# Gated cross-attention with RMS norm on one core: where the last quad's element-wise work and the first quad's weight sums stand in the engines' queues

## The chip, the cores and the metric

The kernel runs on one core of a Trainium2 chip. The metric is the device time in microseconds (us) of one launch; the median of three runs is given, and one further execution was recorded by the profiler. Five engines matter. TensorE (PE in the profile) multiplies matrices, and its weight loads have a row of their own (PEld). VectorE (DVE) and ScalarE (ACT) work element by element and can read the accumulators (PSUM). GpSimd (POOL) works element by element on SBUF. SyncE (SP) issues DMA transfers. Each engine works through its own queue in order, and waits there for what other engines have to finish.

## The reference

```
memory_proj = einsum('bme,de->bmd', memory, W_mem)
scores = einsum('bnd,bmd->bnm', x, memory_proj) / sqrt(D)
memory_context = einsum('bnm,bmd->bnd', softmax(scores), memory_proj)
gate = sigmoid(einsum('bnf,df->bnd', concat([x, memory_context]), W_gate) + b_gate)
fused = x + gate * memory_context
out = fused * rsqrt(mean(square(fused)) + 1e-6) * norm_w
```

Here x is 8 x 1024 x 1024, memory is 8 x 64 x 512, D is 1024, and everything is float32. The first half of W_gate (called W1) is multiplied with x; the second half acts on the attention's output, and its product with memory_proj is made once in a setup stage.

## The kernel before

The 8192 rows of x are taken in 16 groups of 512 rows, here called quads (`NQ` = 16), each of four tiles of 128 rows. The product of a quad with W1 is made as seven smaller products (a Strassen scheme on two levels), in the order 1, 6, 7, 5, 4, 2, 3 of `ORDER` (line 584). Each of the seven is one call of `outer_product` (line 726) and is itself made of seven inner products, called A, B, C, D, A again, E and F. Each inner product is one slot, so a quad has 49 slots. The last four outer products (5, 4, 2, 3) also carry a part of the attention's output and of the gate (`ext`): between the second A and E, TensorE multiplies the attention weights with the memory (tiles pc, and sums into kA, kF, kE and kD).

What comes out of PSUM is taken out as follows. ScalarE copies A to p1 (line 783). VectorE adds B, C and D to make u2, u3 and u4 (lines 785, 787, 791). GpSimd adds u3 and u4 to the gate tiles (`pre`, line 765), and VectorE adds A, D, E and F (`fin`, line 771). In the four products with `ext`, ScalarE then makes the sigmoid of two half tiles of 128 x 512: d, the odd tile of a row pair, after E, and c, the even one, after F. TensorE needs the copy p1 before the second A may add to the same bank, since it adds to what it left there, and it needs u4 before the attention product may add to D's bank.

Work beside these products stands in a table by slot: `at(slot, fn)` (line 577) enters it, and `step()` (line 628) issues what is due right before the slot's inner product. Within one slot, what was entered first is issued first. The order so written is kept on each engine (`pin`). Thus a step that is moved by one slot changes its place in the queues of VectorE and ScalarE against the copies and sums of that slot, and never the order on TensorE.

For the first 15 quads, the product with the memory context is `gated` (line 633); adding x comes from a DMA that accumulates (`residual`), and `square` and `norm` (lines 647 and 660) follow in the next quad. The last quad has no next one, and differs. Its x lies in SBUF as xl. `last_gated` (line 691) multiplies a half tile with pc (which carries the memory context), adds xl, and ScalarE squares it with a sum along the row into one column of `halves` (`junk` takes the squares). `last_root` (line 704) adds the two half sums on VectorE and takes the root on ScalarE; `last_norm` (line 709) takes the reciprocal once per tile, scales a half tile and stores it. In the last quad rows 2 and 3 are finished by products 5 and 4, and rows 0 and 1 by products 2 and 3. Sigmoid and root lie in different tables of ScalarE, so a root between sigmoids has a table load ahead of it and one behind it (rows ACT_TABLE_LOAD); `sqrt_table` (line 721) loads the root's table early in the very end.

The first quad has a part of its own. Four sums of W1 each for products 2 and 3 (`inner_sum`, line 210, 128 x 512 each) are made on VectorE while the first quad runs, at the slots of line 625. Product 2 first needs its sums in slot 36, and product 3 in slot 43. The softmax of the first quad stands in the slots 10 (`softmax_a`) and 13 (`softmax_b`), and slot 18 transposes its result on TensorE (`transpose_attn`, tile pa).

Of the kernel before, what the change touches and what calls it, by code (L numbers as in the profile page):

```python
# [9 lines left out]
AF = mybir.ActivationFunctionType  # L10
ALU = mybir.AluOpType
# [4 lines left out]
P = 128  # L16
# [4 lines left out]
def tile_gated_cross_attention_rmsnorm(  # L21
# [42 lines left out]
    nc = tc.nc  # L64
    B, N, D = x.shape
# [18 lines left out]
    small = ctx.enter_context(tc.tile_pool(name="small", bufs=1))  # L84
# [9 lines left out]
    def tt(eng, o, a, b, op):  # L94
        pin(eng.tensor_tensor(o, a, b, op))  # L95
# [4 lines left out]
    def t4k(pool, shape, tag, name):  # L100
        return pool.tile(shape, F32, tag=tag, name=name)
# [475 lines left out]
    def at(slot, fn, *args):  # L577
        due.setdefault(slot, []).append(lambda: fn(*args))
# [43 lines left out]
    for o in (2, 3):  # L622
        w1_place(o)
    for i, (o, n) in enumerate((o, n) for o in (2, 3) for n in range(4)):
        at((3, 4, 5, 6, 10, 11, 12, 13)[i], inner_sum, nc.vector, o, n)
    slot = 0

    def step():
# [62 lines left out]
    def last_gated(t, h, pc):  # L691
        q = NQ - 1
        gated(q, t, h, pc)
        cols = slice(h * H, (h + 1) * H)
        g = O[q, t][:, cols]
        tt(nc.vector, g, g, xl[t][:, cols], ALU.add)
        if t not in halves:
            halves[t] = t4k(small, [P, 3], f"halves{t}", f"halves{t}")
        junk = t4k(small, [P, H], "junk", f"junk_{t}_{h}")
        pin(  # L700
            nc.scalar.activation(junk, g, AF.Square, accum_out=halves[t][:, h : h + 1])
        )

    def last_root(t):
        ss = halves[t]
        tt(nc.vector, ss[:, 2:3], ss[:, 0:1], ss[:, 1:2], ALU.add)
        pin(nc.scalar.activation(ss[:, 2:3], ss[:, 2:3], AF.Sqrt, bias=eps_sb, scale=1.0 / D))

    def last_norm(t, h):
        b, n0 = where(NQ - 1, t)  # L710
        rstd = halves[t][:, 2:3]
        if h == 0:
            pin(nc.vector.reciprocal(rstd, rstd))
        cols = slice(h * H, (h + 1) * H)
        g = O[NQ - 1, t][:, cols]
        pin(
            nc.vector.scalar_tensor_tensor(g, g, rstd, nw_sb[:, cols], ALU.mult, ALU.mult)  # L717
        )
        load(out[b, n0 : n0 + P, cols], g)
# [6 lines left out]
    def outer_product(q, o, ext):  # L726

        nonlocal slot, banks
        l11, l12, l21, l22 = quarters(left(q, o))
        s1, s2, s3, s4 = (L2[q, o][:, i, :, :] for i in range(4))  # L730
        kb = {}

        def product(name, tag, lhsT, s, start=True):
            nonlocal slot
            step()
            if name not in kb:
                kb[name] = ps.tile([P, C], F32, tag=banks[tag], name=f"k{name}{q}_{o}")
            for k in range(2):
                mm(kb[name], lhsT[:, k, :], w_op(o, s)[:, k, :], start and k == 0, k == 1)
            slot += 1  # L740

        def o_blocks(row, h):

            for t in (2 * row, 2 * row + 1):
                if (q, t) not in O:
                    O[q, t] = t4k(gpool, [P, D], "gate", f"gate{q}_{t}")
            return [
                O[q, 2 * row + r][:, h * H + n * C : h * H + (n + 1) * C]
                for r in range(2)
                for n in range(2)  # L750
            ]


        sums = {
            1: [(o_blocks(0, 0), None)],
            6: [(o_blocks(0, 1), (0, 0))],
            7: [(o_blocks(1, 0), (0, 1))] if o == 7 else [],
            5: [(o_blocks(1, 1), (1, 0)), (o_blocks(0, 1), (0, 1))] if o == 5 else [],
            4: [(o_blocks(1, 0), (1, 0))] if o == 4 else [],
            2: [(o_blocks(0, 0), (0, 0))] if o == 2 else [],  # L760
            3: [(o_blocks(0, 1), (0, 1))] if o == 3 else [],
        }[o]
        sums = [(dst, src and o_blocks(*src)) for dst, src in sums]

        def pre(n, u):

            for dst, src in sums:
                if src is not None:
                    tt(nc.gpsimd, dst[n], src[n], u, ALU.add)

        def fin(n, name, u):
            for dst, src in sums:
                if src is not None:
                    tt(nc.vector, dst[n], (src if u is None else dst)[n], kb[name], ALU.add)
                elif u is not None:
                    tt(nc.vector, dst[n], u, kb[name], ALU.add)
                else:
                    pin(nc.scalar.copy(dst[n], kb[name]))

        ut = t4k(rot, [P, 4, C], "u", f"u{q}_{o}")  # L780
        p1, u2, u3, u4 = (ut[:, i, :] for i in range(4))
        product("A", 0, l11, R11)
        pin(nc.scalar.copy(p1, kb["A"]))  # L783
        product("B", 1, s2, T2)
        tt(nc.vector, u2, p1, kb["B"], ALU.add)
        product("C", 2, s3, R12)
        tt(nc.vector, u3, u2, kb["C"], ALU.add)
        pre(3, u3)
        pre(2, u3)
        product("D", 3, s1, T1)  # L790
        tt(nc.vector, u4, u2, kb["D"], ALU.add)
        pre(1, u4)
        product("A", 0, l12, R21, False)
        pcs = []
        if ext:
            row, h, g = ext
            at_, mg = attnTs[q], mgs[q // QPB]
            for n in ("E", "F"):
                kb[n] = ps.tile([P, C], F32, tag=banks[4 if n == "E" else 1], name=f"k{n}{q}_{o}")
            for r, names in ((0, ("A", "F")), (1, ("E", "D"))):  # L800
                pc = ps_ctx.tile([P, H], F32, tag="ctx", name=f"pc{q}_{o}_{r}")
                for n in range(2):
                    cols = slice(h * H + n * C, h * H + (n + 1) * C)
                    mm(
                        pc[:, n * C : (n + 1) * C],
                        at_[0:M, 2 * row + r, :],
                        mg[0:M, cols],
                        n == 0,
                        True,
                    )  # L810
                    mm(
                        kb[names[n]],
                        at_[M:P, g + r, :],
                        mg[M:P, cols],
                        names[n] in "EF",
                        True,
                    )
                pcs.append(pc)
        for fn in beside.pop((q, o), ()):
            fn()  # L820
        fin(0, "A", None)
        fin(3, "D", u3)
        product("E", 4, l22, T4, not ext)
        fin(2, "E", u3)
        if ext:
            sigmoid(q, 2 * row + 1, h)
            last = q + 1 == NQ
            if last:
                at(slot + 1, last_gated, 2 * row + 1, h, pcs[1])
            else:  # L830
                at(slot + 1, gated, q, 2 * row + 1, h, pcs[1])
        product("F", 1, s4, R22, not ext)
        fin(1, "F", u4)
        if ext:
            sigmoid(q, 2 * row, h)
            if last:
                at(slot + 2, last_gated, 2 * row, h, pcs[0])
            else:
                at(slot + 2, gated, q, 2 * row, h, pcs[0])
        if o in (4, 3) and q + 1 == NQ:  # L840
            c, d = 2 * ext[0], 2 * ext[0] + 1
            if o == 3:
                sqrt_table()
            first = (4, 5) if o == 4 else (3, 3)
            at(slot + first[0], last_root, d)
            at(slot + first[1], last_root, c)
            for i, t in enumerate((d, c)):
                for h_ in range(2):
                    at(slot + first[1] + 1 + 2 * i + h_, last_norm, t, h_)
        elif o in (4, 3):  # L850

            row = ext[0]
            c, d = 2 * row, 2 * row + 1
            for t in (d, c):
                at(slot + 5, residual, q, t)
            if row == 0:
                when = (17, 18, 23, 29, None, None)
            else:
                when = (17, 18, 23, 25, 26, 28)
            at(slot + when[0], square, q, c)  # L860
            at(slot + when[1], square, q, d)
            for w_, (t, h_) in zip(when[2:], ((c, 0), (c, 1), (d, 0), (d, 1))):
                if w_ is None:
                    mid((q + 1, 4), norm, q, t, h_)
                else:
                    at(slot + w_, norm, q, t, h_)
        banks = [banks[i] for i in (2, 3, 0, 4, 1)]
        del L2[q, o]
# [34 lines left out]
```

## Time and profile before

| what | value |
|---|---|
| median of 3 runs | 979.76 us (979.5 to 979.79) |
| the profiled execution, its own time | 979.91 us |
| its span, first to last instruction | 978.1 us |
| mean granted clock of TensorE | 0.997 |
| first quad, TensorE | about 82.7 to 137.5 us |
| last quad, TensorE | about 909.2 to 967.5 us |
| last instruction on VectorE ends | 974.96 us |
| VectorE busy from 939.5 us to the end | 30.7 us |
| ScalarE, GpSimd busy in that stretch | 16.4 us, 15.0 us |

All times inside the kernel are counted from the first instruction of the profiled execution. In a line of the timeline, the first number is the start of a group of like instructions, the second is what it spans, and a number in brackets at the end is idle time of that engine ahead of it, with what ended it. A wait says which engine and tile waited, for whom, how long in total, how often, and the longest. An engine that is idle and isn't the bottleneck costs nothing.

### The profile page before, as it was taken

The numbers are of one execution on the slowest core, as the hardware profiler recorded it, in microseconds if no ns is written. First come the engines' busy times: TensorE is split into PE (matmuls) and PEld (weight loads), VectorE is DVE, ScalarE is ACT, GpSimd is POOL, SyncE is SP. The second block draws the span as 40 slices with busy tenths as digits, with TensorE's granted clock in tenths as the row PEclk, the third lists the DMA queues.
The fourth block names the chain that finished last, engine by engine and source line by source line (L and its number), as shares of the span: only waits on it lengthen the run. The fifth ranks groups of instructions, "written<-read, shape, count | busy, mean of one in ns | idle before, by whom it ended". The sixth has DMA issues, their size and how long they took to land.

```text
span 978.1 us, 14392 instructions
## 1 busy us (share of the span) xinstructions
PE 964.3 (99%) x4986; PEld 776.3 (79%) x4986; DVE 827.0 (85%) x1487; ACT 323.0 (33%) x596; POOL 754.6 (77%) x895
## 2 busy tenths in 40 slices
PE   9999999999999999999999999999999999999995
PEld 8646888888888888888888888888888888888873
DVE  5988788979797988979797988979797988979787
ACT  1000234151423334151423334151423334151434
POOL 4986878878787878878787878878787878878772
PEclk9999999999999999999999999999999999999998
DMA  9856173482818373482819373482818373482612
GB/s 371 267 147 157 27 130 98 114 177 72 176 65 174 117 130 98 112 179 73 176 65 175 113 131 99 112 180 71 177 66 172 116 133 98 111 181 68 169 65 86
DMA packets 71255, 128.32 MB, mean 131 GB/s; under 512 B 12432, under 2 KB 49296, under 8 KB 70928
## 3 DMA queue, kind: packets, MB, share of 16 engines
q1 hardware_dynamic: 61760, 93.34, 35.1%
q0 software_dynamic: 9280, 33.56, 18.6%
q8 instruction: 39, 0.64, 0.3%
q10 hardware_dynamic: 144, 0.52, 0.2%
q14 instruction: 32, 0.26, 0.1%
HBM read 87.56 MB, written 39.85 MB: 130 GB/s over the span
## 4 chain that ended last, share of the span: by engine, by line
PE 95%; DVE 3%; DMA 1%; issue 0%; ACT 0%; POOL 0%; DVEq 0%; ACTq 0%
PE kA L92 19%; PE pc L92 12%; PE kE L92 11%; PE kF L92 10%; PE kD L92 10%; PE kC L92 10%; PE kB L92 10%; PE psT L92 6%; PE pg L92 5%; PE pm L92 3%; DVE gate L95 1%; DMA memq<-in_mem 1%; DVE gate L717 0%; PE pa L427 0%; PE sc L401 0%
## 5 line engine op out<-in xcount | busy, mean ns | idle before, releaser
L95 POOL TENSOR_TENSOR gate<-gate,u 128x256 f32<-128x256 f32 x336 | 270.3, 834 | 116.0 <-DVE u L95 110.4
L639 ACT ACTIVATE gate<-gate 128x512 f32<-128x512 f32 x128 | 79.0, 629 | 400.7 <-DVE gate L95 400.6
L95 POOL TENSOR_TENSOR l<-a 128x256 f32<-128x256 f32 x128 | 128.6, 1004 | 56.3 <-DVE a L95 55.5
L333 DVE STREAM_TRANSPOSE a<-xq 128x512 f32<-128x512 f32 x128 | 138.0, 1100 | 3.2 <-DMA mgd<-mpq 3.2
L92 PE MATMUL pc<-mg,attnT 64*128 64x256 f32 x512 | 127.4, 389 | 0.0
L668 DVE SCALAR_TENSOR_TENSOR gate<-gate,ss,nw_sb 128x512 f32<-128x512 f32 x120 | 126.2, 1061 | 1.1
L92 PE MATMUL kD<-it,l 128*128 128x256 f32 x448 | 115.0, 379 | 0.0
L92 PE MATMUL kB<-it,l 128*128 128x256 f32 x448 | 115.0, 379 | 0.0
L92 PEld LDWEIGHTS pc<-mg,attnT 64*128 64x128 f32 x512 | 90.6, 186 | 29.7 <-issue 21.2
L92 PE MATMUL kA<-w,a 128*128 128x256 f32 x384 | 98.7, 379 | 0.4 <-ACT u L783 0.4
L92 PEld LDWEIGHTS kD<-it,l 128*128 128x128 f32 x448 | 85.1, 190 | 11.6
L92 PEld LDWEIGHTS kB<-it,l 128*128 128x128 f32 x448 | 85.1, 190 | 11.6
L95 DVE TENSOR_TENSOR gate<-gate,pc 128x512 f32<-128x512 f32 x128 | 87.2, 681 | 5.8 <-ACT gate L639 5.8
L95 POOL TENSOR_TENSOR l<-s 128x256 f32<-128x256 f32 x96 | 75.6, 787 | 10.1 <-PE kF L92 10.0
L92 PEld LDWEIGHTS kA<-w,a 128*128 128x128 f32 x384 | 71.6, 190 | 10.2 <-ACT u L783 0.8
L783 ACT COPY u<-kA 128x256 f32<-128x256 f32 x112 | 40.5, 362 | 102.4 <-PE kA L92 100.4
L95 DVE TENSOR_TENSOR u<-u,kB 128x256 f32<-128x256 f32 x112 | 45.6, 407 | 28.2 <-PE kB L92 24.7
L92 PE MATMUL kE<-it,a 128*128 128x256 f32 x256 | 69.0, 392 | 0.0
L92 PE MATMUL kA<-t,s 128*128 128x256 f32 x256 | 67.4, 386 | 0.0
L92 PE MATMUL kF<-w,l 128*128 128x256 f32 x256 | 65.7, 379 | 0.0
L92 PE MATMUL kC<-w,l 128*128 128x256 f32 x256 | 65.7, 379 | 0.0
L653 ACT ACTIVATE junk<-gate 128x1024 f32<-128x1024 f32 x60 | 63.5, 1059 | 1.4 <-DMA gate<-in_x 0.5
(138 smaller groups left out, 2034.2 us busy)
## 6 DMA issues: line engine op xcount, KB each, us to landing
xq<-in_x SPq DMA_DIRECT2D x64, 512.0 KB, 9.7
gate<-in_x POOLq DMA_DIRECT2D x60, 512.0 KB, 8.2
out<-gate SPq DMA_DIRECT2D x60, 512.0 KB, 2.6
w<-in_w_gate_t SPq DMA_DIRECT2D x8, 512.0 KB, 11.0
w<-in_w_gate_t SPq DMA_DIRECT2D x2, 2048.0 KB, 17.0
mg<-mgd SPq DMA_DIRECT2D x16, 256.0 KB, 3.8
mpd<-mpT SPq DMA_DIRECT2D x4, 512.0 KB, 6.5
mgd<-mpq SPq DMA_DIRECT2D x16, 128.0 KB, 4.4
```

The lines of the kernel that those rows point to most:

```text
L92: pin(nc.tensor.matmul(o, lhsT, rhs, start=start, stop=stop, skip_group_check=True))
L95: pin(eng.tensor_tensor(o, a, b, op))
L333: nc.vector.transpose(A[key][:, :, r * P : (r + 1) * P], chunks(xq[q][:, 4 * t : 4 * t + 4, :], KD)[:, half * KH : (half + 1) * KH],)
L639: pin(nc.scalar.activation(g, g, AF.Sigmoid))
L653: nc.scalar.activation(junk, O[q, t], AF.Square, accum_out=ss[:, t % 2 : t % 2 + 1])
L668: nc.vector.scalar_tensor_tensor(g[:, cols], g[:, cols], rstd[:, t % 2 : t % 2 + 1], nw_sb[:, cols], ALU.mult, ALU.mult,)
L783: pin(nc.scalar.copy(p1, kb["A"]))
```

## The change

There are two parts.

In the first quad, the four sums of W1 for product 3 move from the slots 10 to 13 to the slots 22 to 25. The four for product 2 stay.

In the last quad, every `last_gated` comes one slot later: d's moves from the slot of the next product's A to that of its B, and c's from C to D. `halves` keeps which half tile came first. After the square of the first half, ScalarE makes (sum / D + eps) with one more instruction of a single column (Identity), and the root takes that column as its bias and the second half's sum as its input, so VectorE's sum of the two halves falls away. The root of d is issued before the square of c in the very end. The four norms of rows 2 and 3, which stood in four slots one after the other, stand in the slots of A, C, the second A and E of the last product, 3 (offsets 7, 9, 11 and 12, where they were 6 to 9); the roots stay at 4 and 5. For rows 0 and 1, which come after the last product, the offsets only set the order.

The instructions of TensorE, of GpSimd and of the DMA queues keep their number and order. VectorE has four instructions fewer, ScalarE four more; the number of table loads is the same.

```diff
--- before.py
+++ after.py
@@ -622,7 +622,7 @@
     for o in (2, 3):
         w1_place(o)
     for i, (o, n) in enumerate((o, n) for o in (2, 3) for n in range(4)):
-        at((3, 4, 5, 6, 10, 11, 12, 13)[i], inner_sum, nc.vector, o, n)
+        at((3, 4, 5, 6, 22, 23, 24, 25)[i], inner_sum, nc.vector, o, n)
     slot = 0
 
     def step():
@@ -695,20 +695,29 @@
         g = O[q, t][:, cols]
         tt(nc.vector, g, g, xl[t][:, cols], ALU.add)
         if t not in halves:
-            halves[t] = t4k(small, [P, 3], f"halves{t}", f"halves{t}")
+            halves[t] = t4k(small, [P, 3], f"halves{t}", f"halves{t}"), h
+        ss, first = halves[t]
         junk = t4k(small, [P, H], "junk", f"junk_{t}_{h}")
+        pin(nc.scalar.activation(junk, g, AF.Square, accum_out=ss[:, h : h + 1]))
+        if h == first:
+            pin(
+                nc.scalar.activation(
+                    ss[:, 2:3], ss[:, h : h + 1], AF.Identity, bias=eps_sb, scale=1.0 / D
+                )
+            )
+
+    def last_root(t):
+        ss, first = halves[t]
+        h = 1 - first
         pin(
-            nc.scalar.activation(junk, g, AF.Square, accum_out=halves[t][:, h : h + 1])
+            nc.scalar.activation(
+                ss[:, 2:3], ss[:, h : h + 1], AF.Sqrt, bias=ss[:, 2:3], scale=1.0 / D
+            )
         )
-
-    def last_root(t):
-        ss = halves[t]
-        tt(nc.vector, ss[:, 2:3], ss[:, 0:1], ss[:, 1:2], ALU.add)
-        pin(nc.scalar.activation(ss[:, 2:3], ss[:, 2:3], AF.Sqrt, bias=eps_sb, scale=1.0 / D))
 
     def last_norm(t, h):
         b, n0 = where(NQ - 1, t)
-        rstd = halves[t][:, 2:3]
+        rstd = halves[t][0][:, 2:3]
         if h == 0:
             pin(nc.vector.reciprocal(rstd, rstd))
         cols = slice(h * H, (h + 1) * H)
@@ -826,7 +835,7 @@
             sigmoid(q, 2 * row + 1, h)
             last = q + 1 == NQ
             if last:
-                at(slot + 1, last_gated, 2 * row + 1, h, pcs[1])
+                at(slot + 2, last_gated, 2 * row + 1, h, pcs[1])
             else:
                 at(slot + 1, gated, q, 2 * row + 1, h, pcs[1])
         product("F", 1, s4, R22, not ext)
@@ -834,19 +843,18 @@
         if ext:
             sigmoid(q, 2 * row, h)
             if last:
-                at(slot + 2, last_gated, 2 * row, h, pcs[0])
+                at(slot + 3, last_gated, 2 * row, h, pcs[0])
             else:
                 at(slot + 2, gated, q, 2 * row, h, pcs[0])
         if o in (4, 3) and q + 1 == NQ:
             c, d = 2 * ext[0], 2 * ext[0] + 1
             if o == 3:
                 sqrt_table()
-            first = (4, 5) if o == 4 else (3, 3)
-            at(slot + first[0], last_root, d)
-            at(slot + first[1], last_root, c)
-            for i, t in enumerate((d, c)):
-                for h_ in range(2):
-                    at(slot + first[1] + 1 + 2 * i + h_, last_norm, t, h_)
+            when = (4, 5, 7, 9, 11, 12) if o == 4 else (2, 4, 5, 6, 7, 8)
+            at(slot + when[0], last_root, d)
+            at(slot + when[1], last_root, c)
+            for w_, (t, h_) in zip(when[2:], ((d, 0), (d, 1), (c, 0), (c, 1))):
+                at(slot + w_, last_norm, t, h_)
         elif o in (4, 3):
 
             row = ext[0]
```

## Prediction

> **What bounds the kernel now.** I read the page's engine totals first, then the chain that ended last, then the last quad by TensorE's timeline, then VectorE's and ScalarE's there, and the first quad last.
>
> ```profile
> PE 964.3 (99%) x4986; PEld 776.3 (79%) x4986; DVE 827.0 (85%) x1487; ACT 323.0 (33%) x596; POOL 754.6 (77%) x895
> PE 95%; DVE 3%; DMA 1%; issue 0%; ACT 0%; POOL 0%; DVEq 0%; ACTq 0%
> ```
>
> TensorE sets the time; only what shortens its waits, or the work after its last product, can help. VectorE comes second. TensorE's waits in the last quad, from its timeline:
>
> ```profile
> 943.35 1.13 PE L92 MATMUL kA<-t,a 128*128 128x256 f32 x4 [0.17 <-ACT u L783]
> ...
> 952.22 1.13 PE L92 MATMUL kA<-w,a 128*128 128x256 f32 x4 [0.36 <-ACT u L783]
> ...
> 961.82 1.13 PE L92 MATMUL kA<-w,s 128*128 128x256 f32 x4 [1.08 <-ACT u L783]
> ...
> 964.92 0.70 PE L92 MATMUL kD<-mg,attnT 64*128 64x256 f32 x2
> 965.55 1.13 PE L92 MATMUL kE<-it,s 128*128 128x256 f32 x4
> 966.51 1.03 PE L92 MATMUL kF<-w,l 128*128 128x256 f32 x4
> ```
>
> The reader is to see three second A's that wait for ScalarE's copy p1, and one kD that comes late. How much in all: in the first quad, an outer product with attention runs from one A to the next in 8.17 us (113.60 to 121.77). In the last quad the three take 939.56 to 948.24, 948.24 to 957.12, and 957.12 to 967.37 (F's start plus one slot, 0.86). That is 8.68, 8.88 and 10.25, so they wait 0.51 + 0.71 + 2.08 = 3.30 us. Why the copy is late shows on ScalarE:
>
> ```profile
> 954.78 1.28 ACT L707 ACT_TABLE_LOAD   x1
> 956.08 0.72 ACT L707 ACTIVATE halves<-halves,eps_sb 128x1 f32<-128x1 f32 x2
> 956.82 1.28 ACT L639 ACT_TABLE_LOAD   x1
> 958.11 1.25 ACT L639 ACTIVATE gate<-gate 128x512 f32<-128x512 f32 x2
> 960.78 0.63 ACT L701 ACTIVATE junk<-gate 128x512 f32<-128x512 f32 x1 [1.42 <-DVE halves L713]
> ...
> 961.41 0.35 ACT L783 COPY u<-kA 128x256 f32<-128x256 f32 x1
> ```
>
> The copy stands behind the square of d, which waits for d's product and x sum on VectorE, and these stand there behind a norm. PE's A was done at about 958.1. Last, the end, on VectorE:
>
> ```profile
> 970.02 0.69 DVE L95 TENSOR_TENSOR gate<-gate,xl 128x512 f32<-128x512 f32 x1
> 970.89 0.16 DVE L95 TENSOR_TENSOR halves<-halves 128x1 f32<-128x1 f32 x1 [0.17 <-ACT junk L701]
> 971.64 0.16 DVE L95 TENSOR_TENSOR halves<-halves 128x1 f32<-128x1 f32 x1 [0.59 <-ACT junk L701]
> 971.83 0.16 DVE L713 RECIPROCAL halves<-halves 128x1 f32<-128x1 f32 x1
> 972.03 1.42 DVE L717 SCALAR_TENSOR_TENSOR gate<-gate,halves,nw_sb 128x512 f32<-128x512 f32 x2
> ```
>
> VectorE waits for both squares before the first norm. In the first quad, TensorE stops once:
>
> ```profile
> 101.42 1.03 PE L92 MATMUL kD<-it,l 128*128 128x256 f32 x4
> 102.59 0.41 PE L427 MATMUL pa<-ident,e 128*128 128x128 f32 x2
> ```
>
> A slot is 0.86 us, so pa was possible at 102.28: 0.31 us lost. The softmax's last step ended at 102.44 behind W1 sums.
>
> **What the Trainium skill says.** "ScalarE: Activation LUTs", section What ACT_TABLE_LOAD costs: a load takes about 1283 ns, and as much again for a drain. Every load here has 1.28; the root's first use starts at 956.08, 0.02 after it, so I add no drain. Same page, section Table sets: identity is in every set, so the new Identity needs no load; no run here shows that yet. "SBUF — State Buffer", section Who interferes with whom: a VectorE instruction with two SBUF inputs and a GpSimd one that reads SBUF exclude each other, and the second waits. The trace agrees in kind: the W1 sums, 0.68 us alone, took 0.85, 1.23 and 0.88 beside GpSimd's adds; GpSimd's three adds took 2.84 there and 2.10 later.
>
> **First quad.** Four sums leave the softmax's slots: pa's 0.31 us wait goes, and the ScalarE copies after it come earlier too. They land on slots 22 to 25, where VectorE was idle 0.65 + 0.37 + 0.44 us before B, C and D (from 107.4, 108.2, 109.1), and GpSimd busy. I price them at 0.9, 0.6, 0.9 and 1.0 (free ones 0.68 less the 0.08 by which the next overlaps, others with about half a GpSimd add of waiting). With everything 0.31 earlier: the attention difference ends near 106.05, then sum, u2 until 107.45, sum, u3 until 108.4, sum, u4 until 109.65, sum until 110.6. Queued behind are the two transposes (2.06), kA's pair of gate sums and kD's (0.67 each): 114.0. TensorE wants D's bank back for B of the next product at 114.46 - 0.31 = 114.15. So about nothing is lost. If each sum waits for a whole GpSimd add (0.67 + 0.70 = 1.37), kD's pair ends at 115.9 and 1.8 us is lost. GpSimd's six adds wait for u3, as before at about 108.7. Range: gain 0.31, loss 1.5; I take the gain of 0.3.
>
> **Product 4.** The copy leads on ScalarE, so the second A (943.01) doesn't wait. But VectorE's queue from 940.50 has the same eight instructions ahead of u4's end: two pc products, two x sums, a norm, u2, u3, u4, only reordered, and it had no idle time there. u4 ended at 945.73 and will end near 945.85, the second x sum now meeting GpSimd's adds, which u3 starts earlier. TensorE needs kD at A + 5.82 (113.60 to 119.42 in the first quad) = 945.38. It waits; E starts near 946.5 (before 946.41). Gain nothing; at best 0.5.
>
> **Product 2.** Sigmoids unchanged (948.92); the copy follows by 950.0. Second A needs it at 951.7: no wait. VectorE: pc 949.3, x sum to 950.7, u2, u3 after C at 951.4, pc and x sum to 952.9, u4 to 953.3; kD wanted at 954.2. E starts at 948.35 + 6.34 = 954.7 instead of 955.29: gain 0.6.
>
> **Product 3.** A at 956.5. ScalarE: c's square 952.9 to 953.6, table, two roots (0.3 each), table: 956.9, sigmoids to 958.1, copy to 958.4. Second A wants it at 956.5 + 3.45 = 960.0: no wait. The slack of 1.5 us hides two loads, two roots and two Identities (0.20 to 0.36 each, rows of 128x1 on L724 and L707). VectorE from the last gate sum (957.1): reciprocal 0.19, norm 0.67, pc 0.71, x sum 0.61, u2 0.34, norm 0.67, u3 0.34, pc 0.71, x sum 0.61 + 0.3 beside GpSimd, u4 0.41: 962.7. TensorE wants kD at 962.3. It waits 0.4; E at 962.7 + 0.06 + 0.63 (as 964.92 to 965.55) = 963.4, F 964.35 against 966.51. Gain at TensorE's end: 2.2 of 3.3.
>
> **The end.** Behind u4 on VectorE stand a reciprocal, both norms of c, and the gate sums. With GpSimd's last add against one norm, E's gate sum ends at about 965.55, so d's sigmoid starts at 965.6, c's at 966.15 (from 968.10: 1.95 less, not 2.2); then table load and warm root (968.75 to 970.15 before): square of d at 968.2. From it before to the end: 970.15 to 974.96 = 4.81. Now the root follows the square and its accumulator read at once: 0.76, root 0.29, reciprocal 0.23, then the norms' 2.93 (972.03 to 974.96): 4.2. c's square and root (about 1.0) lie beside d's two norms (1.42). VectorE ends at 972.4: 2.55 us earlier. The final stores keep their spacing and landing (2.0 us).
>
> **Sum.** 2.55 + 0.3 = 2.85. 979.91 (span 978.1 and 1.8 around it) - 2.85 = 977.1; the median is 0.15 below this execution. I say 977.0.
>
> **Rivals.** (1) VectorE keeps up everywhere, so all waits go: 3.30 + 0.6 + 0.3 = 4.2, 975.7. For it: VectorE is idle 8 of the last 38.6 us. Against it: the unbroken queue from 940.50. (2) Every wait moves on to kD behind u4: TensorE gains nothing, leaving the end's 0.6 and the first quad's 0.3: 979.0. For it: kD already waits in product 3 (0.45 us of weight load for u4). Against it: product 2's u4 has nearly 1 us to spare. (3) Slower: the shared read port. Four W1 sums and nine two-input steps ahead of u4 in the last quad (norms and x sums) each wait for a whole GpSimd add, 1.37 us instead of my mean 0.82. First quad loses 1.5; product 4 loses 1.4 and product 2 0.3 against my sum, product 3 2.5: 2.2 - 4.2 = -2.0, and the end's 0.4 is left, so the last quad loses 1.6. In all +3.1: 983.0. It decides from a mean of about 1.1. For it: the norms of L668 average 1.06. Against it: that is with GpSimd three quarters busy; in the last quad's rest it works 15.0 of 38.6 us. That the change doesn't do what it says is excluded: the order of the changed program shows the copy ahead of d's square in all three products, and the four sums moved.
>
> **Chances and range.** Forecast 0.65, rival 1 0.17, rival 2 0.13, slower 0.05. A difference under 0.2% (1.96 us) can't be told from none: forecast and rival 1 are faster (0.82), rival 2 same (0.13), rival 3 slower (0.05). The range goes from rival 1's 975.7 to 978.3, a forecast in which the first quad loses 1 us (+1.3); above it lies most of rivals 2 and 3, below it little.
>
> **What would show it.** No wait of a second A for ScalarE's copy; kD waits of about 0.4 us for u4 in products 4 and 3; E of product 3 some 2.2 us earlier; one root between two squares, and VectorE waiting only once between the last x sum and the first norm. pa directly after kD, and B of product 4 in the first quad without a gap. Wrong: a gap of over 0.5 us at that B; u4 of product 3 more than 1 us after TensorE wants it; a table load at the Identity.

## The result, and the profile after

The changed kernel takes 976.1 us (median of 6 runs, 975.96 to 976.7) against 979.68 us for the kernel before, a ratio of 0.9965 with a 95% interval of 0.9952 to 0.9978. A second series of five gave 975.93 us and 0.9962 (0.9950 to 0.9975). So it is about 3.6 us faster, where 2.85 was forecast, and 0.9 us below the 977.0 that I said, near the lower end of the range. The profiled execution has a span of 974.7 us.

TensorE's timeline in the last quad, the rows that answer to those shown of before:

```profile
943.04 1.03 PE L92 MATMUL kA<-t,a 128*128 128x256 f32 x4
...
951.45 1.03 PE L92 MATMUL kA<-w,a 128*128 128x256 f32 x4
...
959.62 1.03 PE L92 MATMUL kA<-w,s 128*128 128x256 f32 x4
...
961.97 0.38 PE L92 MATMUL pc<-mg,attnT 64*128 64x256 f32 x1
962.10 0.48 PE L92 MATMUL kD<-mg,attnT 64*128 64x256 f32 x1
...
962.72 1.13 PE L92 MATMUL kE<-it,s 128*128 128x256 f32 x4
963.69 1.03 PE L92 MATMUL kF<-w,l 128*128 128x256 f32 x4
```

No second A carries an idle time any more: each starts 3.45 to 3.46 us after its first A (3.79, 3.98 and 4.70 before). The one trace of a wait left is kD, in products 4 and 3: here its first product starts 0.13 us after the pc product beside it, where in product 2, without a wait, it is 0.01. It comes when u4 is done on VectorE, at 962.04:

```profile
961.63 0.41 DVE L95 TENSOR_TENSOR u<-u,kD 128x256 f32<-128x256 f32 x1
```

ScalarE ahead of product 3's copy:

```profile
953.80 1.28 ACT L713 ACT_TABLE_LOAD   x1
955.09 0.48 ACT L713 ACTIVATE halves<-halves 128x1 f32<-128x1 f32 x2
955.59 1.28 ACT L639 ACT_TABLE_LOAD   x1
956.88 1.15 ACT L639 ACTIVATE gate<-gate 128x512 f32<-128x512 f32 x2
957.94 0.35 ACT L792 COPY u<-kA 128x256 f32<-128x256 f32 x1
959.07 0.63 ACT L701 ACTIVATE junk<-gate 128x512 f32<-128x512 f32 x1 [0.78 <-DVE gate L95]
```

The copy now follows the sigmoids at once and is done 1.3 us before the second A; the square of d comes behind it, and its wait costs nothing. VectorE at the end:

```profile
967.30 0.69 DVE L95 TENSOR_TENSOR gate<-gate,xl 128x512 f32<-128x512 f32 x1
968.39 0.16 DVE L722 RECIPROCAL halves<-halves 128x1 f32<-128x1 f32 x1 [0.41 <-ACT halves L713]
968.59 1.42 DVE L726 SCALAR_TENSOR_TENSOR gate<-gate,halves,nw_sb 128x512 f32<-128x512 f32 x2
```

From the last x sum's start to the first norm it is 1.29 us, against 2.01 before. On ScalarE, d's root now stands between the two squares:

```profile
968.07 0.29 ACT L713 ACTIVATE halves<-halves 128x1 f32<-128x1 f32 x1
968.27 0.61 ACT L701 ACTIVATE junk<-gate 128x512 f32<-128x512 f32 x1
```

In the first quad, pa stands directly behind kD (TensorE's timeline):

```profile
101.69 1.03 PE L92 MATMUL kD<-it,l 128*128 128x256 f32 x4
102.55 0.38 PE L427 MATMUL pa<-ident,e 128*128 128x128 f32 x2
```

To compare runs I cut each trace into five stretches by the starts of matrix products: in the first quad from A of product 6 to A of product 2; product 4 (A to A); product 2 (A to A); product 3 (A to F); and the end (from F's start to the end of the last norm). Between these, from the first quad's A of product 2 to the last quad's A of product 4, before and after take 817.79 and 817.78 us. The setup ahead of them differs from execution to execution by some tenths: the first quad's second A starts at 86.17 before and 86.44 after.

| kernel | first quad | product 4 | product 2 | product 3 | end | ratio to before (95%) |
|---|---|---|---|---|---|---|
| before | 29.31 | 8.68 | 8.88 | 9.39 | 8.45 | |
| whole change | 29.08 | 8.40 | 8.17 | 7.53 | 7.84 | 0.9965 (0.9952 to 0.9978) |
| a1: W1's sums only | 29.08 | 8.68 | 8.87 | 9.39 | 8.45 | 0.9997 (0.9988 to 1.0005) |
| a2: last_gated later only | 29.29 | 8.41 | 8.17 | 8.52 | 8.45 | 0.9981 (0.9973 to 0.9990) |
| a3: norms spread only | 29.29 | 8.68 | 8.88 | 8.90 | 9.12 | 1.0000 (0.9991 to 1.0008) |
| a4: root only | 29.30 | 9.02 | 8.80 | 9.66 | 7.84 | 0.9997 (0.9989 to 1.0006) |
| a5: whole, norms not spread | 29.09 | 8.42 | 8.17 | 8.51 | 7.84 | 0.9973 (0.9963 to 0.9983) |
| a6: whole, last_gated not moved | 29.08 | 9.03 | 8.81 | 8.96 | 8.34 | 0.9996 (0.9988 to 1.0004) |
| b1: whole, c behind u4 | 29.08 | 8.17 | 8.49 | 9.22 | 7.85 | 0.9983 (0.9976 to 0.9990) |
| b2: b1, fourth sum in slot 33 | 28.97 | 8.17 | 8.47 | 9.23 | 7.85 | 0.9980 (0.9972 to 0.9988) |
| b3: whole, norms behind u4 | 28.96 | 8.40 | 8.17 | 7.31 | 8.33 | 0.9964 (0.9951 to 0.9978) |
| b4: b3, older norm behind u4 | 28.97 | 8.17 | 8.33 | 7.35 | 8.56 | 0.9967 (0.9955 to 0.9980) |

The stretches of the whole change are shorter by 0.23 + 0.28 + 0.71 + 1.86 + 0.61 = 3.69 us. The two spans differ by 3.4, as the setup of this execution took 0.27 longer. The timings alone don't tell a1, a3, a4 and a6 from before (their intervals hold 1), so these rest on the stretches of one profile each. Stretches that an edit leaves alone agree within some 0.02 us from profile to profile, so the differences read below are clear of that.

### The profile page after: what moved, and what is told of

The parts are those of the page before. It is cut to its first block, busy times and chain, and to the rows that moved or that the text cites. A ratio compares the mean times of both kernels' runs of the same rounds, so it can differ in the third digit from the quotient of the medians.

```text
span 974.7 us, 14389 instructions
## 1 busy us (share of the span) xinstructions
PE 963.2 (99%) x4986; PEld 776.9 (80%) x4986; DVE 824.8 (85%) x1483; ACT 323.9 (33%) x600; POOL 755.6 (78%) x895
## 4 chain that ended last, share of the span: by engine, by line
PE 98%; DMA 1%; ACT 0%; DVE 0%; DVEq 0%; issue 0%
PE kA L92 20%; PE pc L92 12%; PE kE L92 11%; PE kD L92 10%; PE kF L92 10%; PE kC L92 10%; PE kB L92 10%; PE psT L92 6%; PE pg L92 5%; PE pm L92 3%; DMA memq<-in_mem 1%; PE sc L401 0%; PE pa L427 0%; PE pt L194 0%; DVE gate L726 0%; ACT L733 0%
```

## The experiments

My theory was that three waits bound the last quad: the copy p1 behind a square on ScalarE, u4 behind norms on VectorE, and the end behind both squares. The rivals were that the norms' place alone makes the waits, that the parts simply add up, and that the read port which VectorE and GpSimd share gives the gain back.

**Each part alone.**

```diff
 a1 -  at((3, 4, 5, 6, 10, 11, 12, 13)[i], inner_sum, nc.vector, o, n)
    +  at((3, 4, 5, 6, 22, 23, 24, 25)[i], inner_sum, nc.vector, o, n)
 a2 -  at(slot + 1, last_gated, 2 * row + 1, h, pcs[1])
    +  at(slot + 2, last_gated, 2 * row + 1, h, pcs[1])
    -  at(slot + 2, last_gated, 2 * row, h, pcs[0])
    +  at(slot + 3, last_gated, 2 * row, h, pcs[0])
 a3 -  norms of rows 2 and 3 at 6, 7, 8, 9
    +  at 7, 9, 11, 12
 a4    last_gated's Identity and last_root as after; roots and norms
    +  when = (4, 5, 6, 7, 8, 9) if o == 4 else (1, 4, 5, 6, 7, 8)
```

> Only the four sums of W1 for product 3 are moved to the slots 22 to 25; the last quad is as before. My theory: in the first quad, the stretch from A of product 6 to A of product 2 (29.31 us before) shortens by 0.2 to 0.3 us, because pa no longer waits for the softmax, and the last quad's three products and end stay at 8.68, 8.88, 9.39 and 8.45 us. In all 0.2 to 0.3 us faster, less than a measurement can tell. Rival (the shared port): the stretch is no shorter, because B of product 4 waits by as much as pa gains.

It came so: 0.23 us in the stretch and nothing elsewhere. Little is given back: the stretch around pa (product 7, A to second A) is 0.34 us shorter, and TensorE needs 1.83 us from A to C of product 4 (1.73 before), so about 0.1 of the 0.34 is lost again.

> Only every last_gated comes one slot later; norms, roots and W1 sums as before. My theory: the waits of the second A for the copy p1 vanish in all three products, since only the place of the copy on ScalarE makes them. Product 4 goes from 8.68 to about 8.4, product 2 from 8.88 to 8.2. In product 3 all four norms still stand ahead of u4 on VectorE, so kD waits for it longer: from A to F about 8.6 us (9.39 before, 7.53 after the whole change). The end stays at 8.45 less what the norms no longer behind u4 free, 8.2. In all about 2 us faster. Rival (the norms' place makes the waits): the second A of product 3 still waits 1 us or more, and in all less than 1 us is gained.

The waits for the copy are gone in all three products (each second A starts 3.45 us after its first), and 1.87 us of stretches agree with the ratio 0.9981 (1.86). Only the end didn't shorten. In product 3 all four norms stand ahead of u4, and kD comes when u4 (VectorE) is done:

```profile
962.51 0.41 DVE L95 TENSOR_TENSOR u<-u,kD 128x256 f32<-128x256 f32 x1
```

```profile
962.98 0.70 PE L92 MATMUL kD<-mg,attnT 64*128 64x256 f32 x2
```

The first is a2's VectorE, ending at 962.92; the second its TensorE, which could have begun at about 961.87 (A at 956.05 and 5.82 on).

The edit moves two things at once: the square on ScalarE, and its product and x sum on VectorE. No run moves one without the other. That the copy is what counts is read from the traces and has no run of its own: all three second A's wait for it before, and none does here.

> Only the four norms of rows 2 and 3 are spread over product 3 (offsets 7, 9, 11, 12); last_gated, roots and W1 sums as before. My theory: nothing changes in product 4 (8.68) and product 2 (8.88), and in product 3 the second A still waits for the copy behind d's square, by 0.5 to 1.2 us; two norms fewer ahead of u4 take away most of the wait of kD. From A to F 8.6 to 9.2 us (9.39 before). In all 0.2 to 0.8 us faster. Rival (the norms make the waits): the second A no longer waits in product 3, from A to F at most 8.0 us, more than 1.4 us faster.

Product 3 gained 0.49, inside the expectation, but the end lost 0.67, which I had not expected, and the time stayed. The two norms that left the place ahead of u4 now stand ahead of the gate sums (a3's VectorE):

```profile
965.93 1.24 DVE L717 SCALAR_TENSOR_TENSOR gate<-gate,halves,nw_sb 128x512 f32<-128x512 f32 x1
967.09 0.41 DVE L95 TENSOR_TENSOR gate<-gate,kE 128x256 f32<-128x256 f32 x1
967.42 0.41 DVE L95 TENSOR_TENSOR gate<-gate,kF 128x256 f32<-128x256 f32 x1
```

F's gate sum starts 1.45 us after F (1.14 before), 0.31 later. E's starts 2.09 us after E (1.23 before), so d's sigmoid is late too, and behind the gate sums VectorE waits 0.36 us for it, where it did not before. The product behind them starts 2.22 us after F (1.48 before), and 0.67 of these 0.74 us reach the end:

```profile
968.19 0.69 DVE L95 TENSOR_TENSOR gate<-gate,pc 128x512 f32<-128x512 f32 x1 [0.36 <-ACT gate L639]
```

The rival's form, that the second A no longer waits, is refuted too: it starts at A + 4.20.

> Only the root's new form (Identity, then the root with it as bias, no sum on VectorE) and d's root ahead of c's square in the end; last_gated, norms and W1 sums as before. My theory: the end shortens by 0.6 us, from 8.45 to about 7.85, and product 3 by 0.1 to 0.3 us, because the roots between the sigmoids no longer wait for VectorE's sums; product 4 and 2 stay. In all 0.6 to 0.9 us faster. Rival (the Identity costs a table load or delays the copy): product 3 gets longer by 0.2 us or more and the end gains less than 0.3.

The end gained the 0.61 it was to gain; how much of it is the Identity's and how much the new place of d's root, no run separates. But products 4 and 3 became longer by 0.34 and 0.27, against my expectation: the Identity delays the copy that stands behind it (product 2 has none ahead of its copy, and gained 0.08). a4's ScalarE:

```profile
961.27 0.18 ACT L701 ACTIVATION_READ_ACCUMULATOR junk<-gate 128x1 f32 x1
961.49 0.29 ACT L704 ACTIVATE halves<-halves,eps_sb 128x1 f32<-128x1 f32 x1
961.69 0.35 ACT L792 COPY u<-kA 128x256 f32<-128x256 f32 x1
```

There is no table load at L704; the cost is 0.04 us of waiting and 0.29 of work, on the path because d's square and Identity lie ahead of the copy. So the second half of the rival holds for the products, and the first half of the theory for the end.

The four alone sum to 0.23 + 1.87 - 0.16 + 0.09 = 2.03 us, well short of 3.69. The parts don't add up; they enable one another.

**All parts but one.**

```diff
 a5 -  when = (4, 5, 7, 9, 11, 12) if o == 4
    +  when = (4, 5, 6, 7, 8, 9) if o == 4
 a6 -  at(slot + 2, last_gated, 2 * row + 1, h, pcs[1])
    +  at(slot + 1, last_gated, 2 * row + 1, h, pcs[1])
    -  at(slot + 3, last_gated, 2 * row, h, pcs[0])
    +  at(slot + 2, last_gated, 2 * row, h, pcs[0])
    -  else (2, 4, 5, 6, 7, 8)
    +  else (1, 4, 5, 6, 7, 8)
```

> The whole change, but the four norms of rows 2 and 3 stand at the offsets 6 to 9 as before. My theory: products 4 and 2 keep their 8.40 and 8.17 us and the end its 7.84, but in product 3 kD waits for u4 behind all four norms, as it did with last_gated moved alone: from A to F 8.5 us instead of 7.53. So 1.0 us slower than the whole change, some 2.6 us faster than before. Rival (the spread only carries norms from ahead of u4 to behind it, as it did alone, where product 3 gained 0.49 and the end lost 0.67): F is 1 us later and the end 0.7 us shorter, and nearly nothing is lost.

It came so: product 3 takes 8.51 and all else is as in the whole change. The spread is worth 0.98 us here, and was worth nothing alone.

> The whole change, but every last_gated in its slot of before. My theory: the copy again stands behind d's square, and now behind the Identity too, so product 4 takes 9.0 us, product 2 8.8 and product 3 9.1 from A to F, and the end 8.2, two norms standing there behind u4; in all within 0.5 us of before, though three of the four parts are in. Rival (the parts add up): it is faster than before by all that the whole change gains but the 1.85 us of last_gated moved alone, that is by 1.8 us.

Three of four parts bring 0.0004 of the time, and the interval includes no gain; the stretches say 0.5 us, not the 1.8 that adding up would leave. Without the later `last_gated` the second A's wait for the copy again, the Identity stands ahead of the copy, and two norms stand behind u4 in the end. So the order of causes is: the later `last_gated` first, worth 1.87 us alone; the rest gives 0.49 without it and 1.82 on top of it.

**Going on.** The late kD still costs products 4 and 3 about 0.23 us each: they take 8.40 and 7.53, where 8.17 and 7.31 are reached without that wait. Four attempts to remove this, and the 0.1 in the first quad:

```diff
 b1 -  at(slot + 3, last_gated, 2 * row, h, pcs[0])
    +  at(slot + 4, last_gated, 2 * row, h, pcs[0])
    -  else (2, 4, 5, 6, 7, 8)
    +  else (3, 5, 6, 7, 8, 9)
 b2    b1, and
    +  at((3, 4, 5, 6, 22, 23, 24, 33)[i], inner_sum, nc.vector, o, n)
 b3    the whole change, slot 33 as in b2, and
    +  when = (4, 5, 7, 11, 11, 13) if o == 4
 b4    b3, and for the quad before
    -  when = (17, 18, 23, 29, None, None)
    +  when = (17, 18, 23, 32 if q + 2 == NQ else 29, None, None)
```

> The whole change, and c's last_gated one slot later still, behind u4 on VectorE. My theory: the last waits of kD for u4 go, product 4 takes 8.17 us instead of 8.40, and product 3 7.30 from A to F instead of 7.53; VectorE then has a product and an x sum more behind u4, but nothing to wait for there, and F's gate sum follows TensorE at 1.13 us as before, so the end stays near 7.84 to 8.1. In all 0.2 to 0.45 us faster than the whole change. Rival (VectorE sets the end of product 3): the end grows by the 0.45 that TensorE gains, and the time stays.

Both theory and rival were wrong. Product 4 did gain its 0.23, but product 2 lost 0.32 and product 3 lost 1.69. In product 2 the weight load of B waits 0.45 us for kD's gate sum of product 4, which is done at 948.74 instead of 948.09: c's x sum behind u4 takes 1.08 us instead of 0.72, and the two norms after it 2.34 instead of 2.02. For product 3, b1's waits of the weight loads, its TensorE, and its VectorE name the cause:

```profile
PEld pc L92 <- DVE gate L95: 2.1, 1, 2.1
```

```profile
963.39 0.48 PE L92 MATMUL pc<-mg,attnT 64*128 64x256 f32 x1 [1.65 <-DVE gate L95]
```

```profile
962.66 0.68 DVE L95 TENSOR_TENSOR gate<-gate,pc 128x512 f32<-128x512 f32 x1
```

The pool of pc has two banks. Product 3's second pc needs the bank of product 2's, which c's last_gated reads; that reading ended at 963.34, and pc began 0.05 us later. In the whole change the same reading ends at 960.96 and that pc begins at 961.54, so 0.6 us is all the room there was:

```profile
960.28 0.68 DVE L95 TENSOR_TENSOR gate<-gate,pc 128x512 f32<-128x512 f32 x1
```

```profile
961.54 0.38 PE L92 MATMUL pc<-mg,attnT 64*128 64x256 f32 x1
```

> As the kernel with c's last_gated behind u4, and in the first quad the fourth of the moved sums of W1 stands in slot 33 instead of 25, behind the gate sums of product 5. My theory: B of product 4 in the first quad no longer waits, since one sum of 0.8 us less stands ahead of kD's gate sums: from A of product 6 to A of product 2 28.98 us instead of 29.08. In all 0.1 us faster than that kernel, too little for a timing; it shows in the stretch alone. Rival (GpSimd's late adds make that wait): the stretch stays at 29.08.

The first-quad stretch came to 28.97, as the theory said: the fourth sum ahead of the gate sums is the 0.1 us that B's bank costs. The rest repeats b1.

> The whole change, with the fourth moved sum of W1 in slot 33, and in product 3 only one norm (d's first half) ahead of u4; d's second and c's first half stand behind u4 and c's second half behind E's gate sum. My theory: kD no longer waits in product 3 (7.30 from A to F), c's product with pc is read 0.7 us earlier, so no attention product waits for its bank; E's and F's gate sums follow TensorE, so the end stays at 7.84 to 7.9; the first-quad stretch is 28.97. In all 0.2 to 0.35 us faster than the whole change. Rival (VectorE behind u4 sets the end): the end grows by the 0.23 us that TensorE gains, 0.1 us is left.

The rival was right in kind, and the end lost more than it said. TensorE gained its 0.22 (product 3 at 7.31), and the end grew by 0.49. b3's VectorE:

```profile
963.39 0.41 DVE L95 TENSOR_TENSOR gate<-gate,kE 128x256 f32<-128x256 f32 x1
963.73 0.74 DVE L726 SCALAR_TENSOR_TENSOR gate<-gate,halves,nw_sb 128x512 f32<-128x512 f32 x1
964.39 0.41 DVE L95 TENSOR_TENSOR gate<-gate,kF 128x256 f32<-128x256 f32 x1
```

F's gate sum comes 1.63 us after F instead of 1.13. From u4 to the last sum VectorE never waits.

> As the kernel before it, and the norm of the quad before that stands ahead of u4 in product 4 goes behind it. My theory: kD no longer waits in product 4 either (8.17 us), and nothing that follows is later: 0.5 us faster than the whole change in all. Rival: product 2's B waits for kD's gate sum behind three norms, as it did when c's last_gated stood behind u4 (product 2 took 8.49), and nothing is gained.

Product 4 gained 0.23 and product 2 gave back 0.16, the end 0.23 more than b3: no gain either. Neither b3 nor b4 beats the whole change by a measurable amount, and by their stretches (3.54 and 3.33 us against 3.69) they are behind it. W1's fourth sum in slot 33 alone on the whole change wasn't run.

The whole change was run again beside them:

> The whole change once more, beside the two kernels that go on from it. Expected: 3.4 to 3.7 us faster than before; first-quad stretch 29.08 us, products 8.40, 8.17 and 7.53, end 7.84.

It gave 29.09, 8.39, 8.16, 7.54 and 7.84, within 0.01 us of the first profile.

## Why the prediction was right, step by step

Set against the stretches, the forecast of 2.85 us was 0.84 short of the 3.69 measured: the first quad was put 0.07 too high, and products 4, 2 and 3 and the end 0.28, 0.11, 0.26 and 0.26 too low. So between the stretches hardly anything cancels: the waits of the last quad were named where they were, and four of the five sizes were too cautious.

**First quad**, 0.3 forecast, 0.23 measured. pa's wait went, and the bank for B of product 4 cost 0.1 rather than nothing. The four sums took 1.10, 0.68, 0.68 and 0.88, together 3.03 with the overlap taken off, against 3.4 reckoned in the same way; but the first of them began some 0.6 later than I had put it, the longer setup taken off, as the attention difference ahead of it took 0.80 us (0.48 before). These two misses nearly cancel. b2, with one sum moved away, gets the 0.1 back.

**Product 4**, 0 forecast, 0.28 measured. The mechanism was as told (no wait for the copy, then one for u4), but u4 was done at 945.49, not 945.85: the two x sums took 0.69 and 0.72 (1.07 and 0.69 before), and I had reckoned with GpSimd's adds in their way; the norm took 1.09, 1.22 before. Only the size was off.

**Product 2**, 0.6 forecast, 0.71 measured: all of its wait, the difference being product 4's tenth.

**Product 3**, 1.6 forecast (2.2 at TensorE's end less 0.6), 1.86 measured. kD wanted at 961.98 began at 962.10, 0.12 late where I had put 0.4. Again the x sum beside GpSimd took 0.72, not 0.9. The slack that was to hide two loads and two roots was there (the copy is done 1.3 us early). My two Identities do not draw on it: those of product 3 stand behind its copy, at 959.83 and 962.50. In a4, where an Identity stands ahead of the copy, it costs 0.3 us each time.

**The end**, 0.35 forecast, 0.61 measured. The chain from d's square to the end was 4.20 (967.33 to 971.53), as reckoned, against 4.81; this alone is the 0.61. What I had taken off for VectorE's queue did not arise: F's gate sum starts at F + 1.13, E's was late by 0.2 without delaying c's sigmoid. b3 shows that this was near: one norm more there and the end grows.

**The rivals.** That all waits go (975.7) was nearest to the time, but kD still waits twice, so the forecast's mechanism stood and its contention terms were too large. That every wait moves on to kD is refuted: TensorE's three stretches are 2.85 us shorter. The shared port didn't decide: nine two-input steps ahead of u4 took 0.69 to 1.09 us, 0.78 in the mean, against the mean of about 1.1 at which it would have. The Trainium skill, "SBUF — State Buffer", section Who interferes with whom, says that the order of issue decides which of the two waits. The trace fits this: GpSimd's three adds in product 3 took 3.05 us beside VectorE's x sum of 0.72 and norm of 0.75, and 2.10 before. By these lengths GpSimd did most of the waiting, and it had time; they do not show which of each pair was issued first. What the Trainium skill, "ScalarE: Activation LUTs", section Table sets, says of identity, that it is in every set, fits too: no load stands ahead of the Identity at L704. The loads cost 1.28 us each, and what follows starts 0.01 us behind them (955.09, 956.88), as reckoned.

What the prediction lacked was a resource: it never asked when c's product with pc must be read so that the next product's pc can have its bank. It held with 0.6 us to spare, and since it was not asked, that was luck.

## What to carry to other kernels

Where an in-order engine carries both the copy that the matrix engine waits for and work that waits for another engine, issue the copy first; here a move of one slot was worth 1.87 us alone, and the rest was worth 0.49 without it and 1.82 on top of it. Try such parts in combination, since a step that lies on the path alone (the Identity, the norms behind u4) can be free once another is moved. And when moving a step that reads an accumulator, look up who gets its bank next: one slot more cost 1.7 us.

## What the runs showed of the hardware that was not expected

A short ScalarE instruction that reads an accumulator just read out started 0.04 us after the readout's end and took 0.29 us, so 0.33 us for one column of numbers, nearly as much as a copy of 256 (0.35). The 0.29 lies inside the 0.20 to 0.36 reckoned for it; that it would lie ahead of a copy that TensorE waits for, I had not put into my expectation of a4. And a VectorE product of 128x256 in the first quad's softmax took 1.68 us beside GpSimd's adds in the changed kernel, where the same one took 0.42 before; TensorE did not wait for it. It came again in every run with W1's sums moved (1.68 to 1.70) and in none that leaves them (0.42), so here it was VectorE that lost 1.26 us.
